# Layer statistics taken behind the additions that finish x, in a block of twelve sublayers

## The chip, the cores and the metric

The kernel runs on one core of one Trainium2 chip. The metric is the device time in microseconds (us). The core has five engines that work side by side, each through its own queue of instructions in order: PE (matrix products and transposes), DVE (vector operations), ACT (activation functions, each from a table that has to be loaded), POOL (general vector work) and SP (which here only issues transfers). They wait for one another through semaphores. On-chip data lie in SBUF, and what PE writes lies in PSUM. An array holds 128 rows (partitions); a tile is 128 tokens.

## What is computed

A perceiver-like stack of four levels, each with a cross attention to a context of 1601 tokens, an attention among the 64 tokens of a sequence, and a feed-forward layer. The twelve sublayers differ (slot attention with a GRU cell, random-feature attention, mixtures of experts, a quantised product at the end), but all are joined in one way:

```python
def _layernorm(x, axis=-1, eps=1e-05):
    m = jnp.mean(x, axis=axis, keepdims=True)
    v = jnp.var(x, axis=axis, keepdims=True)
    return (x - m) / jnp.sqrt(v + eps)

    # x: (16, 64, 256) float32
    x = x + _L1_xattn_ref(_layernorm(x, axis=-1), ctx_1024, ...)
    x = x + _L1_attn_ref(_layernorm(x, axis=-1), ...)
    x = x + _L1_ffn_ref(_layernorm(x, axis=-1), ...)
    ...
```

So every sublayer needs mean and variance of each of 1024 rows of 256 numbers, and these are known only when the sublayer before has added its result to x.

## The kernel before

x stays in SBUF through all layers, as `self.x` of shape 128 x 8 x 256: eight tiles of 128 tokens. The layers are methods that run one after the other: `l0_xattn`, `l0_attn`, `l0_ffn`, `l1_xattn` and so on to `l3_attn`, which carries the last feed-forward layer in its loop. Each layer adds its result to x tile by tile. In l1_attn, l2_xattn, l2_attn and l3_xattn this is `add_to_x` (line 358, DVE, out of PSUM). In l1_xattn it is an addition on POOL in `end` (line 1320). In l1_ffn it is a DVE addition in `refine` (line 1690), and in l2_ffn a multiply-and-add per expert in `weighted_experts` (line 879), of which the last expert's finishes x.

At its head a layer normalises x, per tile: `bn_stats` and `bn_aggr` on DVE give mean and variance; `rstd` makes the factor out of the variance with a tensor_scalar on DVE (line 133, variance plus eps), Sqrt on ACT (line 134) and a reciprocal on DVE (line 135), for two or four tiles at a time; another tensor_scalar writes the norm, (x - mean) * factor, to `xln` (in l1_ffn to `xi`). PE then transposes the norm, DVE and ACT in turn copy the transposes from PSUM to `xT` (lines 124 and 126; cT in l1_ffn), and the layer's first product (`lin_t`, `lin` or `gelu_t`) reads that.

The heads that matter here: `linear` in `token_attention` (line 2488 on), which serves l1_attn and l3_attn and takes the tiles in two halves of four; `start` in l1_ffn (line 1552), also by halves; `layernorm` (line 138), called by l2_xattn and l2_ffn for all eight tiles; `linear` in l2_attn (line 1829); `prepare` in l3_xattn (line 2048).

Some other instructions stand in the neighbourhood. `token_attention` clears its array `vm` with a POOL memset (line 2491), fills the small array `ones` (lines 2494 and 2496), and POOL later adds the norm and a bias row to x (lines 2524 and 2525). In l3_attn the product `pb` (line 2202) and 32 small additions `bias` (line 2212) make the position bias. In l2_xattn's streamed loop DVE masks the scores (line 1779), ACT squares them (lines 1781 and 1782) and POOL adds up some of the exponent's results, `tot` (line 2385). In l2_attn's loop over tiles, DVE makes `kp` (line 1910), `rec` (lines 1941 and 1942) and `kv` (lines 1925 and 1926), and POOL scales `qp` once (line 1896).

What sets the order: in the layers here, PE's instructions and some others that are marked with `pin` keep the order of the program. All others, the statistics, factors and norms among them, are placed by a planner, which goes by costs of its own and by when operands are due; so the order on DVE, ACT and POOL can differ from that of the code. The compiled order is what the prediction goes by.

Of the kernel before, what the change touches and what calls it, by code (L numbers as in the profile page):

```python
# [64 lines left out]
class Sections:  # L65
# [21 lines left out]

    def c(self, name):
        lo, n = CONSTS_AT[name]
        return self.cst[:, lo : lo + n]  # L90
# [37 lines left out]
    def rstd(self, pool, var, eps, tag, scale=1.0):  # L128
# [7 lines left out]
        return r  # L136

# [732 lines left out]
    def weighted_experts(self, ps, sb2, xT, comb, n, hidden, down):  # L870

        nc = self.nc
        for e in range(n):
# [4 lines left out]
            def evac(t, pm):  # L878
                nc.vector.scalar_tensor_tensor(
                    self.x[:, t, :], pm, comb[:, t, e : e + 1], self.x[:, t, :], ALU.mult, ALU.add  # L880
                )

# [128 lines left out]
    def l1_xattn(self):  # L1011
# [3 lines left out]
        with ExitStack() as ctx:  # L1015
# [301 lines left out]
            def end(step, after):  # L1317
                s, i = step
                if i == 2:
                    pin(nc.gpsimd.tensor_tensor(self.x[:, s.t, :], self.x[:, s.t, :], s.s, ALU.add))  # L1320
                if after and after[1] == 0:
# [29 lines left out]
            for n in range(len(a)):  # L1351
# [12 lines left out]
                else:  # L1364
                    for x in sb_.p:
                        x.exp()
                        x.weigh()
                update(sb_, an and an[0])
# [91 lines left out]
    def l1_ffn(self):  # L1460
# [3 lines left out]
        with ExitStack() as ctx:  # L1464
# [214 lines left out]
            def refine(s):  # L1679
                fT = sb.tile([P, 4, N], F32, tag=f"eT{s.i}", name="fT")  # L1680
                for c in range(4):
                    gelu_t(fT[:, c, :], fw1, s.cT, self.v(k + "refine_b1")[:, c : c + 1], KC, c * P)
                for t in range(TT):
# [6 lines left out]
                    nc.vector.tensor_tensor(s.x[:, t, :], s.x[:, t, :], y, ALU.add)  # L1690

# [36 lines left out]
    def l2_xattn(self):  # L1728
        nc, tc, d = self.nc, self.tc, self.d
        with ExitStack() as ctx:  # L1730
# [10 lines left out]
            self.layernorm(sb, self.x, xln)  # L1741
# [46 lines left out]
            def out(t):  # L1788
# [3 lines left out]
                self.add_to_x(t, pm)  # L1792

            self.stream(ps, sb2, load, wkv[:, :, :D], wkv[:, :, D:], copy, weights, finish, out)

    def l2_attn(self):
        nc, tc, d = self.nc, self.tc, self.d
        F, HT = 64, NT // 2
        with ExitStack() as ctx:
# [27 lines left out]
            def linear(i):  # L1827
# [993 lines left out]
```

## Time and profile before

| | |
|---|---|
| median of 3 runs | 3760.18 us (3752.28 to 3766.32) |
| profiled execution | 3753.96 us |
| its span | 3752.2 us |
| PE busy | 3440.3 us, 92% |
| DVE busy | 1974.1 us, 53% |
| ACT busy | 1451.3 us, 39% |
| POOL busy | 1291.0 us, 34% |
| granted TensorE clock, mean | 0.959 |

Times in the profile are microseconds from the start of the span. A line of the timeline has the start, the busy time, the engine, the line of the code, the operation, the arrays (out<-in) with their shapes, the number of instructions put together in the line (x), and in brackets the idle time before it and what ended it. Operations of l1_xattn run up to 1917 us, l1_attn to 2005, l1_ffn to 2333, l2_xattn to 2996, l2_attn to 3103, l2_ffn to 3467, l3_xattn to 3621, and l3_attn from there.

### The profile page before, as it was taken

Reading aid. Unit: us, or ns where it says so; the run is one execution under the profiler, and the core shown is the slowest. Engines: PE = TensorE matmul, PEld = TensorE weight load, DVE = VectorE, ACT = ScalarE, POOL = GpSimd, SP = SyncE. Lnnn points to the kernel's source line nnn. Section 1 sums busy time; section 2 is a strip of 40 time slices with the busy share of each in tenths; the row PEclk is TensorE's granted clock in tenths of the full one; section 3 lists DMA queues with packets and bytes.
Section 4 is the critical chain, followed back from the end, with each engine's and each line's share of the span. In section 5 each row is a group of like instructions: output and inputs, shape, how many; then the busy total and the mean of one; then the engine's idle time right before and its main releaser. Section 6 shows DMA issues by size and latency. Waiting matters only on the chain.

```text
span 3752.2 us, 70803 instructions
## 1 busy us (share of the span) xinstructions
PE 3440.3 (92%) x30966; PEld 2187.8 (58%) x30966; DVE 1974.1 (53%) x3676; ACT 1451.3 (39%) x2076; POOL 1291.0 (34%) x787
## 2 busy tenths in 40 slices
PE   8999999996999969999977988999999789999986
PEld 4555555563665645555545666667767555555554
DVE  5344333436555546656657554577767665333346
ACT  2333333333444414444423443466666612111213
POOL 1555555562011123333321001577777630000012
PEclk9999999998999979999989999999999989999997
DMA  4111001101332344343101001111111004111640
GB/s 145 38 38 38 31 27 38 38 10 35 105 96 87 111 158 163 127 146 110 37 26 40 1 6 44 68 56 38 56 38 38 11 2 174 43 36 30 278 180 13
DMA packets 106123, 258.66 MB, mean 69 GB/s; under 512 B 9203, under 2 KB 74483, under 8 KB 103510
## 3 DMA queue, kind: packets, MB, share of 16 engines
q1 hardware_dynamic: 97366, 222.68, 16.6%
q10 hardware_dynamic: 6912, 27.27, 2.3%
q8 instruction: 243, 3.98, 0.4%
q0 software_dynamic: 1536, 4.20, 0.4%
q14 instruction: 66, 0.54, 0.0%
HBM read 248.34 MB, written 5.77 MB: 68 GB/s over the span
## 4 chain that ended last, share of the span: by engine, by line
PE 77%; DVE 12%; ACT 7%; issue 2%; DMA 1%; POOL 1%; SPq 0%; ACTq 0%; DVEq 0%; POOLq 0%
PE sc L2452 15%; PE pk L2452 15%; PE lin L2452 7%; PE acc L2452 6%; PE lin_t L2452 5%; ACT e L327 5%; PE pu L2452 4%; PE lin L194 3%; PE gate L2017 3%; PE up L2017 3%; PE pc L1639 3%; PE prz L2452 2%; PE gelu_t L1549 2%; PE turn L2457 2%; PE pa L2452 1%
## 5 line engine op out<-in xcount | busy, mean ns | idle before, releaser
L2385 POOL TENSOR_TENSOR tot<-tot,e 128x1024 f32<-128x1024 f32 (+1 forms) x340 | 802.9, 2361 | 374.5 <-ACT e L327 251.2
L270 DVE TENSOR_REDUCE m<-sc 128x4 f32<-128x2048 f32 x96 | 220.1, 2293 | 271.3 <-PE sc L2452 270.2
L1779 DVE SCALAR_TENSOR_TENSOR e<-sc,row_L_xattn_nbias,free 128x2048 f32<-128x2048 f32 x104 | 244.3, 2349 | 121.8 <-PE sc L2452 116.3
L1781 ACT ACTIVATE e<-e 128x2048 f32<-128x2048 f32 x104 | 198.7, 1910 | 243.2 <-DVE e L1779 243.2
L327 ACT ACTIVATE e<-sc 128x2048 f32<-128x2048 f32 x104 | 195.2, 1877 | 241.2 <-PE sc L2452 239.6
L2452 PE MATMUL sc<-qb,kT 32*128 32x128 f32 x6656 | 244.8, 283 | 36.6 <-DVE m L284 12.3
L2452 PEld LDWEIGHTS sc<-qb,kT 32*128 32x128 f32 x6656 | 205.9, 187 | 80.6 <-issue 24.5
L2452 PE MATMUL acc<-e,v 128*32 128x128 f32 x6656 | 226.6, 276 | 6.4 <-ACT e L1782 6.4
L2452 PEld LDWEIGHTS acc<-e,v 128*32 128x32 f32 x6656 | 170.3, 110 | 105.7 <-issue 95.1
L2452 PE MATMUL pk<-cT,wk 128*128 128x512 f32 (+1 forms) x512 | 207.0, 534 | 3.6 <-DVE rows L300 3.6
L2452 PE MATMUL pk<-wv,cT 128*128 128x256 f32 x832 | 209.8, 394 | 0.0
L1782 ACT ACTIVATE e<-e 128x2048 f32<-128x2048 f32 x104 | 198.7, 1911 | 3.3
L2452 PE MATMUL pk<-cT,wkv 128*128 128x512 f32 (+1 forms) x512 | 197.2, 526 | 0.0
L2452 PE MATMUL pk<-wkv,cT 128*128 128x256 f32 x832 | 196.3, 386 | 0.0
L2452 PEld LDWEIGHTS pk<-wv,cT 128*128 128x128 f32 x832 | 149.7, 190 | 75.5 <-issue 58.2
L2452 PEld LDWEIGHTS pk<-wkv,cT 128*128 128x128 f32 x832 | 153.3, 190 | 28.3 <-issue 4.3
L1639 PE MATMUL pc<-ew,eh 128*128 128x256 f32 x640 | 158.8, 391 | 0.0
L2452 PE MATMUL pu<-cn,e 128*64 128x257 f32 (+1 forms) x1248 | 146.5, 391 | 12.9 <-POOL e L1186 12.9
L2452 PE MATMUL sc<-kT,qb 32*128 32x512 f32 (+2 forms) x1536 | 140.8, 465 | 14.9 <-DVE m L270 2.3
L2021 ACT ACTIVATE g<-gate 128x512 f32<-128x512 f32 x68 | 40.6, 597 | 292.2 <-PE gate L2017 292.2
L1176 POOL TENSOR_TENSOR e<-e,mx 128x512 f32<-128x512 f32 x96 | 81.8, 883 | 194.7 <-DVE mx L1175 194.7
L2022 DVE TENSOR_TENSOR hT<-up,g 128x512 f32<-128x512 f32 x68 | 47.0, 692 | 178.8 <-PE up L2017 174.6
(519 smaller groups left out, 6339.5 us busy)
## 6 DMA issues: line engine op xcount, KB each, us to landing
cT<-in_ctx_t SPq DMA_DIRECT2D x128, 832.0 KB, 6.1
cn<-in_ctx_n SPq DMA_DIRECT2D x32, 1664.0 KB, 12.6
piece<-in_ctx_n ACTq DMA_DIRECT2D x32, 640.0 KB, 3.9
w<-in_L_attn_W SPq DMA_DIRECT2D x8, 1024.0 KB, 7.2
piece<-in_ctx_n ACTq DMA_DIRECT2D x16, 384.0 KB, 3.5
w<-in_L_ffn_W SPq DMA_DIRECT2D x16, 256.0 KB, 4.8
down<-in_L_ffn_w_down SPq DMA_DIRECT2D x16, 256.0 KB, 2.7
gate<-in_L_ffn_w_gate SPq DMA_DIRECT2D x16, 256.0 KB, 2.7
```

Of the source, the lines that this page charges most:

```text
L194: nc.tensor.matmul(pm, xT[:, k, t * P : (t + 1) * P], w[:, k, :], start=(k == 0), stop=(k == kc - 1))
L270: nc.vector.tensor_reduce(x.m4[:, g, :, i], pm, AX.X, ALU.max)
L327: nc.scalar.activation(e, pm, AF.Exp, scale=0.25)
L1176: pin(nc.gpsimd.tensor_tensor(p.e, p.e, p.mx.unsqueeze(2).to_broadcast(p.shape), ALU.subtract))
L1549: nc.tensor.matmul(pm, w[:, c, lo : lo + m], cT[:, c, :], start=(c == 0), stop=(c == nk - 1))
L1639: nc.tensor.matmul(pc[:, n, j, :], s.eh[i][:, c, tok], ew2[:, c, cols], start=False, stop=(c == 3))
L1779: nc.vector.scalar_tensor_tensor(e16, pm16, nb, free[:, at : at + P].unsqueeze(1).to_broadcast([P, 16, P]), ALU.add, ALU.mult)
L1781: nc.scalar.activation(e, e, AF.Relu)
L1782: nc.scalar.activation(e, e, AF.Square)
L2017: nc.tensor.matmul(pm[-1], w[:, k, n * P : (n + 1) * P], xT[:, k, tok], start=(k == 0), stop=(k == KC - 1))
L2385: nc.gpsimd.tensor_tensor(tot[:w], x.first if c == 1 else tot[:w], e[:w], ALU.add)
L2452: ins = self.nc.tensor.matmul(*args, **kw)
```

## The change

Two arrays are kept for the whole run: `xm` (mean and variance of each tile) and `xr` (the factors). `measured(t)` takes the statistics of tile t of x and is called directly behind the addition that finishes this tile, in seven layers. `factors(lo, hi)` makes the factors of some tiles. Unless told otherwise, measured calls it for two tiles whenever the second of a pair is done; in l1_xattn, l1_attn and l3_xattn tiles 0 to 5 are done at once behind tile 5, and in l1_ffn tiles 0 to 3 in the second half's refine. `normed(t, to)` writes the norm. The seven layers behind lose their statistics and call normed only. In token_attention the memset of vm is moved, in the code, behind the first half's transposes.

```diff
+        self.xm = self.const.tile([P, NT, 2], F32, tag="xm", name="xm")
+        self.xr = self.const.tile([P, NT], F32, tag="xr", name="xr")
...
+    def measured(self, t, root=True):
+
+        nc = self.nc
+        st = self.const.tile([P, 6], F32, tag="x_st", name="x_st", bufs=2)
+        nc.vector.bn_stats(st, self.x[:, t, :])
+        nc.vector.bn_aggr(self.xm[:, t], st)
+        if root and t % 2:
+            self.factors(t - 1, t + 1)
+
+    def factors(self, lo, hi):
+        nc = self.nc
+        r = self.xr[:, lo:hi]
+        nc.vector.tensor_scalar(r, self.xm[:, lo:hi, 1], 1.0, 1e-5, ALU.mult, ALU.add)
+        nc.scalar.activation(r, r, AF.Sqrt)
+        nc.vector.reciprocal(r, r)
+
+    def normed(self, t, to):
+        self.nc.vector.tensor_scalar(to, self.x[:, t, :], self.xm[:, t, 0:1], self.xr[:, t : t + 1], ALU.subtract, ALU.mult)
... weighted_experts (l2_ffn)
+                if e == n - 1:
+                    self.measured(t)
... l1_xattn
                     pin(nc.gpsimd.tensor_tensor(self.x[:, s.t, :], self.x[:, s.t, :], s.s, ALU.add))
+                    self.measured(s.t, s.t == NT - 1)
...
+                    self.factors(0, NT - 2)
... l1_ffn, start and refine
-                mv = sb2.tile([P, TT, 2], F32, tag="ln_mv", name="ln_mv")
                 for t in range(TT):
-                    st = sb2.tile([P, 6], F32, tag="ln_st", name="ln_st", bufs=3)
-                    nc.vector.bn_stats(st, s.x[:, t, :])
-                    nc.vector.bn_aggr(mv[:, t, :], st)
-                r = self.rstd(sb2, mv[:, :, 1], 1e-5, "ln_r")
-                for t in range(TT):
-                    nc.vector.tensor_scalar(
-                        s.xi[:, t, :], s.x[:, t, :], mv[:, t, 0:1], r[:, t : t + 1], ALU.subtract, ALU.mult)
+                    self.normed(s.i * TT + t, s.xi[:, t, :])
...
+                if s.i:
+                    self.factors(0, TT)
...
                     nc.vector.tensor_tensor(s.x[:, t, :], s.x[:, t, :], y, ALU.add)
+                    self.measured(s.i * TT + t, s.i == 1)
... l2_xattn and l2_ffn, head
-            self.layernorm(sb, self.x, xln)
+            for t in range(NT):
+                self.normed(t, xln[:, t, :])
... l2_xattn and l2_attn, output
                 self.add_to_x(t, pm)
+                self.measured(t)
... l3_xattn, output
                 self.add_to_x(s.t, pm)
+                self.measured(s.t, s.t > 5)
+                if s.t == 5:
+                    self.factors(0, 6)
... token_attention (l1_attn, l3_attn); the heads of l2_attn and l3_xattn change in the same way, but have no memset
-        nc.gpsimd.memset(vm, 0.0)
...
-            mv = sb2.tile([P, HT, 2], F32, tag="ln_mv", name="ln_mv")
-            for t in range(HT):
-                st = sb2.tile([P, 6], F32, tag="ln_st", name="ln_st", bufs=3)
-                nc.vector.bn_stats(st, x[:, t, :])
-                nc.vector.bn_aggr(mv[:, t, :], st)
-            r = self.rstd(sb2, mv[:, :, 1], 1e-5, "ln_r")
...
-                    nc.vector.tensor_scalar(
-                        xln[:, t + j, :], x[:, t + j, :], mv[:, t + j, 0:1], r[:, t + j : t + j + 1],
-                        ALU.subtract, ALU.mult)
+                    self.normed(i * HT + t + j, xln[:, t + j, :])
...
+            if i == 0:
+                nc.gpsimd.memset(vm, 0.0)
...
             self.add_to_x(t, pm)
+            if then is None:
+                self.measured(t, t > 5)
+                if t == 5:
+                    self.factors(0, 6)
```

More of the change, by code (lines that the diff above doesn't have):

```diff
@@ L1950, in project @@
                 self.add_to_x(t, pm)
+                self.measured(t)
             self.pinned = True
@@ L1986, in l2_ffn @@
             xT = sb.tile([P, KC, T], F32, tag="xT", name="xT")
-            self.layernorm(sb, self.x, xln)
+            for t in range(NT):
+                self.normed(t, xln[:, t, :])
             self.transpose(ps, xln, xT)
@@ L2049, in prepare @@
                 xln = sb.tile([P, HT, D], F32, tag="xln", name="xln")
-                mv = sb2.tile([P, HT, 2], F32, tag="ln_mv", name="ln_mv")
-                for t in range(HT):
-                    st = sb2.tile([P, 6], F32, tag="ln_st", name="ln_st", bufs=3)
-                    nc.vector.bn_stats(st, x[:, t, :])
-                    nc.vector.bn_aggr(mv[:, t, :], st)
-                r = self.rstd(sb2, mv[:, :, 1], 1e-5, "ln_r")
                 xT = sb.tile([P, KC, 512], F32, tag="xT", name="xT")
@@ L2059, in prepare @@
                     for j in range(2):
-                        nc.vector.tensor_scalar(
-                            xln[:, t + j, :], x[:, t + j, :], mv[:, t + j, 0:1], r[:, t + j : t + j + 1],
-                            ALU.subtract, ALU.mult)
+                        self.normed(i * HT + t + j, xln[:, t + j, :])
                         for c in range(KC):
@@ L2504, in linear @@
             xln = sb.tile([P, HT, D], F32, tag=f"xln{i}", name="xln")
-            mv = sb2.tile([P, HT, 2], F32, tag="ln_mv", name="ln_mv")
-            for t in range(HT):
-                st = sb2.tile([P, 6], F32, tag="ln_st", name="ln_st", bufs=3)
-                nc.vector.bn_stats(st, x[:, t, :])
-                nc.vector.bn_aggr(mv[:, t, :], st)
-            r = self.rstd(sb2, mv[:, :, 1], 1e-5, "ln_r")
             xT = sb.tile([P, KC, 512], F32, tag=f"xT{i}", name="xT")
@@ L2514, in linear @@
                 for j in range(2):
-                    nc.vector.tensor_scalar(
-                        xln[:, t + j, :], x[:, t + j, :], mv[:, t + j, 0:1], r[:, t + j : t + j + 1],
-                        ALU.subtract, ALU.mult)
+                    self.normed(i * HT + t + j, xln[:, t + j, :])
                     for c in range(KC):
```

## The prediction

> **What bounds the kernel now.** I read the head of the page first, for the size of things, then the shares of the chain of waits, then the timeline around each of the seven places where one layer ends and the next normalises x.
>
> ```profile
> span 3752.2 us, 70803 instructions
> PE 3440.3 (92%) x30966; PEld 2187.8 (58%) x30966; DVE 1974.1 (53%) x3676; ACT 1451.3 (39%) x2076; POOL 1291.0 (34%) x787
> ...
> PE 77%; DVE 12%; ACT 7%; issue 2%; DMA 1%; POOL 1%; SPq 0%; ACTq 0%; DVEq 0%; POOLq 0%
> ```
>
> PE is the bound; only some 300 us of the span are PE idle. The change takes nothing from PE, so it can win only in the short stretches where PE stands still at a layer's head. At the seven heads, from the last addition to the first product that needs the transposed norm, they are 5 to 14 us long and partly filled. Half a percent, about what a measurement of this kernel can tell from no change, is 18.8 us.
>
> Timeline, head of l1_attn. POOL's memset of vm runs 3.51 us, and a DVE instruction on 4 numbers per partition takes 2.15 us beside it; the same one takes 0.15 us alone (at 3468.85, for instance). The transposes wait for the norm, lin_t for the copy behind it.
>
> ```profile
> 1917.50 3.51 POOL L2491 MEMSET vm<- 128x4096 f32 x1
> 1918.98 2.15 DVE L133 TENSOR_SCALAR ln_r<-ln_mv 128x4 f32<-128x4 f32 x1
> 1922.47 4.03 DVE L2515 TENSOR_SCALAR xln<-x,ln_mv,ln_r 128x256 f32<-128x256 f32 x6
> 1922.91 1.97 PE L2457 MATMUL tr<-cst,xln 128*128 128x128 f32 x8 [8.79 <-DVE xln L2515]
> 1927.25 2.05 PE L2452 MATMUL lin_t<-xT,wqkv 128*128 128x512 f32 x2 [2.37 <-DVE xT L124]
> ```
>
> Timeline, end of l2_xattn and the token loop of l2_attn. POOL adds exponentials 2.43 us each without a pause; the copy L2311 takes 1.60 us beside them and 0.29 without. In l2_attn POOL has two instructions of 5.4 us back to back (the boundary is at 3073.1), and the addition to tile 1 falls into the second; kp behind it releases PE's pk.
>
> ```profile
> 2963.43 12.14 POOL L2385 TENSOR_TENSOR tot<-tot,e 128x1024 f32<-128x1024 f32 x5
> 2969.25 1.60 DVE L2311 TENSOR_TENSOR xT<-half 128x128 f32<-128x128 f32 x1
> 2993.49 0.29 DVE L2311 TENSOR_TENSOR xT<-half 128x128 f32<-128x128 f32 x1
> 3067.70 10.81 POOL L1896 TENSOR_SCALAR qp<-qp 128x2048 f32<-128x2048 f32 x2 [11.53 <-ACT qp L1895]
> 3074.13 0.42 DVE L358 TENSOR_TENSOR x<-lin,x 128x256 f32<-128x256 f32 x1 [0.58 <-PE lin L2452]
> 3075.33 1.23 DVE L1910 TENSOR_SCALAR kp<-pkp 128x1024 f32<-128x1024 f32 x1 [0.77 <-PE pkp L2452]
> 3076.61 1.98 PE L2452 MATMUL pk<-va,kp 64*128 64x33 f32 x32
> ```
>
> Timeline, end of l3_xattn. The memset runs ten microseconds before the last addition, hurting nobody. pb starts when that addition is done; 32 small DVE additions follow pb, then the copy, then lin_t.
>
> ```profile
> 3607.17 3.51 POOL L2491 MEMSET vm<- 128x4096 f32 x1 [6.76 <-DMA hot<-in_buckets]
> 3617.54 0.15 POOL L2494 MEMSET ones<- 128x64 f32 x1 [6.86 <-PE pa L2452]
> 3620.18 0.42 DVE L358 TENSOR_TENSOR x<-lin,x 128x256 f32<-128x256 f32 x1 [1.97 <-PE lin L2452]
> 3620.66 6.41 PE L2202 MATMUL pb<-emb,hot 32*128 32x16 f32 x128 [0.52 <-DVE x L358]
> 3629.41 4.53 DVE L2212 TENSOR_TENSOR bias<-pb,cst 64x64 f32<-64x64 f32 x32
> 3634.80 2.90 PE L2452 MATMUL lin_t<-xT,wqkv 128*128 128x512 f32 x3 [5.83 <-DVE xT L124]
> ```
>
> **The rule that speaks against the change.** The row says 0.15 us for a factor instruction. The Trainium skill ("SBUF — State Buffer", section "Who interferes with whom") says that a DVE tensor_scalar between SBUF tiles in a two-port mode, or a DVE operation with two SBUF inputs, shares one pair of ports with GpSimd: whoever starts first keeps it for the whole instruction and the other stands still. The rows above agree (2.15 against 0.15, 1.60 against 0.29), and a reciprocal (L2303, 1.75 us with or without POOL) or an operation out of PSUM is spared. The old code did such work in heads where POOL is mostly idle; the new code puts factors() and normed() where POOL is busy. By the row alone the sum below would be 18.6 us of gain; by the rule it is 3. I take the rule, place by place.
>
> **Part by part.** No instruction is new in kind: 56 bn_stats (0.31 to 0.39 us), 56 bn_aggr (0.08 behind another) and the norms (0.33 to 0.36) are only moved; the factors become pairs or (0,6)+(6,8), some dozen more small DVE and ACT operations. PE's instructions are the same, but for local order in l1_ffn, l2_xattn and l2_ffn. No DMA is added; SP swaps five weight and context loads in l2_ffn, far ahead of their use.
>
> l1_xattn to l1_attn: in the loop bn_stats waits for POOL's addition (0.72 us) with den or sr behind it on DVE; 3.2 us of DVE idle lie there (waiting for pu), so I charge 0.3. In the head, the memset was moved down in the code, but in the compiled order POOL still runs it right behind the addition, before the first norm. So the norms, ready at 1918.0, start at 1921.2; five of them (1.8), the copy (0.7), and lin_t comes at 1924.05 instead of 1927.25, because the copy now stands ahead of the norm that POOL's x+=xln (2.44) blocks. +3.2 - 0.3 = +2.9.
>
> l1_attn to l1_ffn: bn_stats and bn_aggr, 0.4 a tile, in a loop where DVE idles 0.26 to 2.8 a tile: 0.4 in all; the reciprocal of (0,6) waits for ACT's Sqrt table (load 1.28, from 1999.70) with rec of tile 7 behind it: 0.5. In the head xi starts at 2006.1 instead of 2009.51; the fifth stands behind POOL's addition to 2010.2, and gelu_t starts at 2011.3 instead of 2014.62: 3.3. The planner also reorders the control part of l1_ffn (bias preparation later, routing earlier), which I count as 0, bounds -2 and +2. Sum +2.4.
>
> l1_ffn to l2_xattn: two more table loads (2.56) inside refine hide behind PE's gelu products; DVE needs 1.95 a tile against PE's 1.73, so the last addition is 0.45 late. All eight norms follow at once: lin_t at 2338.8 instead of 2344.5, of which 3.4 were PE work (pk) that now comes behind it: +2.3.
>
> l2_xattn to l2_attn: the factor of (0,1) falls into a POOL addition (to 2959.85) with the reciprocal and the exponent's input L1779 behind it, for which ACT and then PE wait: -2.0. That of (2,3), between the two half operations, waits about 1; the copy L2311 then meets the next POOL addition: about -2 more. In the head the four norms follow L2311 directly, without 3.4 us of statistics, 2.3 us of lock at 3000.24 and a second Sqrt: +4.2. Sum 0 (bounds -4 and +4).
>
> l2_attn to l2_ffn: DVE is the bound of this loop (busy without a gap 3079 to 3091, 5.3 us a tile), so what is added counts in full: tiles 0 and 1 0.4 each ahead of kp; tiles 2 to 5 0.4 each, less 0.5 of slack, plus 0.3 for each of two pairs of factors: 1.7. The factor of (0,1), ready at 3075.0, waits for POOL's qp to 3078.5: 3.5, with kp, and so PE's pk, behind it. Sum -6.0. The head begins 2.4 earlier, but all eight norms now stand before the first copy, and ACT drops one Sqrt load: +1.6. Sum -4.4 (bounds -7 and 0).
>
> l2_ffn to l3_xattn: additions come every 0.865, taking 0.48; 0.4 of statistics and at times 0.3 of factors fit, POOL is idle. First norm 3467.4; the copy of two tiles to 3469.6, the fourth norm, ACT's copy, lin_t at 3471.25 instead of 3474.06: +2.8.
>
> l3_xattn to l3_attn: the loop has idle DVE (0). But the memset is now behind ones on POOL, which waits for the last pa: it runs 3617.7 to 3621.2, just when six norms stand in DVE's queue ahead of the last addition. Five end at 3623.0, the sixth waits for POOL's x+=row (2.45) to 3625.4, the addition ends at 3625.8 instead of 3620.6, and pb, bias (needs all of pb) and lin_t follow: pb to 3632.3, bias to 3636.8, copy 0.7, lin_t 3637.7: -3.0 (without the lock +2.1).
>
> Sum: 2.9+2.4+2.3+0-4.4+2.8-3.0 = +3.0 us. From the profiled execution's 3754.0 (span 3752.2 and 1.8 around it) that is 3751.0; it lies 6.2 below the median of the runs, 3760.2, inside their 3752.3 to 3766.3. The forecast for the median is 3757.
>
> **Rivals.** *Faster:* the locks fall elsewhere (POOL a few us earlier or later, in l2_attn above all) and the cheap rows hold: l1_attn 5.9, l1_ffn 2.4, l2_xattn 2.3, l2_attn 4.2, l2_ffn -1.1, l3_xattn 2.8, l3_attn 2.1, together 18.6: 3741.6, and PE staying clocked up over the shorter gaps (its products run at half pace for some 4 us at 1927 and 3474) could add 1 or 2 a head: 3735. Against it: the blocked rows above. *Slower:* bn_stats behind POOL's addition in l1_xattn. If that addition has the multiplications of the other half (three of 1.04 and one of 0.40) ahead of it, DVE stands 3.5 us in each of 8 tiles with den and sr behind it: 28 us, 3785. It decides from 2.7 us a tile on. For it: POOL is pinned and busy there; against it: in the last tile they end at 1902.6, and the addition comes at 1916.84. *The change doesn't do what it says:* that is so for the memset, and is in the sum; would it run behind the transposes after all, the last head gains 5 and the first 2.5: 3750.
>
> **How the numbers follow.** Little change, 0.76; the locks missing, or clock gained, so that over 0.5% is won, 0.16; the l1_xattn stall or more blocked places, over 0.5% lost, 0.08. The bounds of the places (5 of them by 2 to 4 us) combine to about 8, the scatter of the runs is 7: near 3757 that is 3744 to 3770; to leave out no more than 2 in 10 I reach towards both rivals: 3739 to 3775.
>
> **What would show it.** In the changed kernel's timeline: a factor instruction of 3 us or more near 3075, one of 1 to 2 us near 2958; the memset between ones and the first norm at both heads; the last addition of l3_xattn some 5 us after its product; lin_t of l3_xattn 4.5 us after the last addition. The prediction is wrong if the factor instructions are all near 0.15 us (faster), or bn_stats in l1_xattn has idle over 2 us before it that POOL ends (slower).

## The result, and the profile after

The changed kernel takes 3751.9 us (median of 16 runs, 3748.7 to 3758.3) beside 3758.6 us of the kernel before (16 runs, 3752.0 to 3766.4). The ratio is 0.9981, with a 95% interval of 0.9972 to 0.9989: a gain of 0.1 to 0.3%, under the half per cent that I had set as the bound of "no change". The forecast was 3757 and "little change"; the forecast gain was 3.0 us, and 6.7 came.

The page of the changed kernel shows the bound where it was: PE is busy for 92% of the span, as before, and DVE has 10 us more, among them the instructions that stand still beside POOL (called locked in what follows).

```profile
span 3753.9 us, 70772 instructions
PE 3443.9 (92%) x30951; PEld 2189.3 (58%) x30966; DVE 1983.8 (53%) x3682; ACT 1452.0 (39%) x2079; POOL 1292.3 (34%) x787
...
PE 76%; DVE 13%; ACT 7%; issue 3%; POOL 1%; DMA 0%; another core or an unknown queue 0%; SPq 0%; ACTq 0%; DVEq 0%; POOLq 0%
```

This profiled execution is not shorter than the one before (span 3753.9 against 3752.2). It was 3.2 us late when it came to the first head, before any head had changed. The shift arises near 1411, where l1_xattn begins, and is 3.46 or 3.47 us at the additions of that layer's first seven tiles and 3.18 at the last. It is not the change: from the layer's first `qT` to its first addition to x the old kernel took 115.9 us in one profile and 119.1 in another, the changed one 119.6 here. So what follows compares stretches, not spans.

Timeline of the changed kernel, head of l1_attn (start, busy time, engine, line, operation, arrays). POOL starts the memset of vm 0.41 us ahead of the first norm, and the norm, which takes 0.38 without it, stands 3.34. lin_t comes 7.28 us after the last `s` of l1_xattn is written; before it was 10.49.

```profile
1920.77 3.51 POOL L2527 MEMSET vm<- 128x4096 f32 x1
1921.18 3.34 DVE L158 TENSOR_SCALAR xln<-x,xm,xr 128x256 f32<-128x256 f32 x1
1924.53 0.38 DVE L158 TENSOR_SCALAR xln<-x,xm,xr 128x256 f32<-128x256 f32 x1
...
1927.22 1.22 PE L2465 MATMUL lin_t<-xT,wqkv 128*128 128x512 f32 x1 [0.68 <-ACT xT L129]
```

Timeline, end of l2_xattn. One factor instruction stands 1.91 us beside POOL's additions, a second one 0.72, and the copy behind it meets the next addition and stands 2.26 us (0.29 alone). The exponent's input, L1802, waits behind it, then ACT 4.60, then PE 4.32. In the profile before, where this copy stood 1.60, PE waited 2.41 at the same place (last line).

```profile
2953.95 1.91 DVE L153 TENSOR_SCALAR xr<-xm 128x2 f32<-128x2 f32 x1
2967.00 0.72 DVE L153 TENSOR_SCALAR xr<-xm 128x2 f32<-128x2 f32 x1
2968.01 2.26 DVE L2324 TENSOR_TENSOR xT<-half 128x128 f32<-128x128 f32 x1
2970.19 2.34 DVE L1802 SCALAR_TENSOR_TENSOR e<-sc,row_L_xattn_nbias,free 128x2048 f32<-128x2048 f32 x1
2972.56 1.91 ACT L1804 ACTIVATE e<-e 128x2048 f32<-128x2048 f32 x1 [4.60 <-DVE e L1802]
2972.58 2.09 PE L2465 MATMUL sc<-qb,kT 32*128 32x128 f32 x32 [4.32 <-DVE e L1802]
```

```profile
2973.17 1.84 PE L2452 MATMUL sc<-qb,kT 32*128 32x128 f32 x32 [2.41 <-DVE e L1779]
```

Timeline, tile 1 of l2_attn. The factor instruction starts inside POOL's second qp and ends with it, at 3078.4; kp ends with it, and PE's pk waits 2.03 us for kp.

```profile
3067.58 10.81 POOL L1912 TENSOR_SCALAR qp<-qp 128x2048 f32<-128x2048 f32 x2 [15.85 <-ACT qp L1911]
3074.30 0.42 DVE L380 TENSOR_TENSOR x<-lin,x 128x256 f32<-128x256 f32 x1 [0.58 <-PE lin L2465]
3075.44 2.97 DVE L153 TENSOR_SCALAR xr<-xm 128x2 f32<-128x2 f32 x1
3076.59 1.82 DVE L1926 TENSOR_SCALAR kp<-pkp 128x1024 f32<-128x1024 f32 x1
3078.49 3.40 PE L2465 MATMUL pk<-va,kp 64*128 64x33 f32 x32 [2.03 <-DVE kp L1926]
```

Timeline, end of l3_xattn. The memset stands behind `ones`; a cast, a small addition and six norms are held beside it and beside POOL's row addition, and the last addition to x starts 5.99 us after its product does (1.17 us before the change). pb, bias and lin_t follow.

```profile
3614.77 3.51 POOL L2527 MEMSET vm<- 128x4096 f32 x1
3614.97 3.39 DVE L2239 CAST identb<-cst 128x128 bf16<-128x128 f32 x1
3615.18 6.96 DVE L158 TENSOR_SCALAR xln<-x,xm,xr 128x256 f32<-128x256 f32 x6
3616.06 1.13 PE L2465 MATMUL lin<-wv,hT 128*128 128x256 f32 x4 [0.52 <-ACT hT L2159]
3622.05 0.41 DVE L380 TENSOR_TENSOR x<-lin,x 128x256 f32<-128x256 f32 x1
3622.52 7.33 PE L2215 MATMUL pb<-emb,hot 32*128 32x16 f32 x128 [5.33 <-DVE x L380]
3635.30 2.04 PE L2465 MATMUL lin_t<-xT,wqkv 128*128 128x512 f32 x2 [3.56 <-DVE xT L127]
```

The stretches from the first head to the end in one table (us; read off the timelines, from start to start where nothing else is said; plus is a gain). "Before" and "after" are the profiled executions of the two kernels. The prediction's terms stand in the same order. The marks are instructions by the name of the array that they write: an exponent input is the mask operation on DVE that writes `e` (L1802; there are seven in the tail), the last `rec` is L2315, and the second `z` is the second addition to `z` in l2_attn (L1880).

| stretch | before | after | gain | predicted |
|---|---|---|---|---|
| l1_attn head: last s written to lin_t | 10.49 | 7.28 | +3.2 | +3.2 |
| l1_attn loop: lin_t to last addition | 77.34 | 78.14 | -0.8 | -0.9 |
| l1_ffn head: last addition to gelu_t | 10.03 | 5.56 | +4.5 | +3.3 |
| l1_ffn loop: gelu_t to last addition | 317.69 | 319.22 | -1.5 | -0.45 |
| l2_xattn head: last addition to lin_t | 12.20 | 7.65 | +4.6 | with the next row +2.75 |
| l2_xattn loop: lin_t to the seventh last exponent input | 605.26 | 607.94 | -2.7 | |
| l2_xattn tail: from there to the last rec | 40.83 | 44.29 | -3.5 | -4 |
| l2_attn head: rec to the second z | 16.68 | 12.34 | +4.3 | +4.2 |
| l2_attn, second z to addition of tile 1 | 66.85 | 71.94 | -5.1 | -0.8 |
| l2_attn, additions of tile 1 to 7 | 28.14 | 33.11 | -5.0 | -5.2 |
| l2_ffn head: last addition to router product | 5.53 | 3.96 | +1.6 | +1.6 |
| l2_ffn loop: router product to last addition | 358.43 | 357.60 | +0.8 | 0 |
| l3_xattn head: last addition to lin_t | 7.83 | 4.41 | +3.4 | +2.8 |
| l3_xattn loop: lin_t to last transposes | 144.00 | 141.73 | +2.3 | 0 |
| l3_attn head: last transposes of l3_xattn to lin_t | 16.74 | 20.19 | -3.5 | -3.0 |
| l3_attn, lin_t to the end | 117.35 | 118.60 | -1.3 | none |

The heads repeat within 0.4 us in the other profiles of these two kernels, which come below; the loops do not, and the last row lies between 113 and 119 in fourteen profiles, in no order by kernel.

The one large row that I had not seen coming is the stretch in l2_attn ahead of tile 1's addition. Only the statistics of tile 0 are new in it, yet it took 5.1 us longer, all of it in PE's own busy time: 56.9 against 51.6 us for the same products. The experiments begin with the rows that were foreseen and then turn to that one. Single edits here move the whole by a few microseconds, and the intervals of all variants of the changed kernel but one overlap that of the change as made (0.9972 to 0.9989). What they show, they show in the stretches.

### The profile page after: what moved, and what is told of

It is laid out like the page before. It is cut to its first block, busy times and chain, and to the rows that moved or that the text cites. A ratio compares the mean times of both kernels' runs of the same rounds, so it can differ in the third digit from the quotient of the medians.

```text
span 3753.9 us, 70772 instructions
## 1 busy us (share of the span) xinstructions
PE 3443.9 (92%) x30951; PEld 2189.3 (58%) x30966; DVE 1983.8 (53%) x3682; ACT 1452.0 (39%) x2079; POOL 1292.3 (34%) x787
## 4 chain that ended last, share of the span: by engine, by line
PE 76%; DVE 13%; ACT 7%; issue 3%; POOL 1%; DMA 0%; another core or an unknown queue 0%; SPq 0%; ACTq 0%; DVEq 0%; POOLq 0%
PE sc L2465 15%; PE pk L2465 15%; PE lin L2465 7%; PE acc L2465 6%; PE lin_t L2465 5%; ACT e L349 4%; PE pu L2465 4%; PE gate L2035 3%; PE up L2035 3%; PE lin L216 3%; PE pc L1658 3%; PE prz L2465 2%; PE turn L2470 2%; PE gelu_t L1575 2%; PE pa L2465 1%
## 5 line engine op out<-in xcount | busy, mean ns | idle before, releaser
L1802 DVE SCALAR_TENSOR_TENSOR e<-sc,row_L_xattn_nbias,free 128x2048 f32<-128x2048 f32 x104 | 244.3, 2349 | 115.6 <-PE sc L2465 114.0
L2465 PE MATMUL sc<-cT,qT 128*64 128x512 f32 (+1 forms) x768 | 141.9, 522 | 3.6 <-ACT scs L1180 3.1
```

Source lines behind the costliest of these rows:

```text
L1802: nc.vector.scalar_tensor_tensor(e16, pm16, nb, free[:, at : at + P].unsqueeze(1).to_broadcast([P, 16, P]), ALU.add, ALU.mult)
L2465: ins = self.nc.tensor.matmul(*args, **kw)
```

## Experiments

The theory is that what the change wins at the heads it gives back where its small instructions meet POOL (factors in l2_xattn and l2_attn, norms beside the memset). The rivals are that the statistics in the loops cost what is missing, whatever POOL does, and, for l2_attn, that the new order makes PE slow.

### The factors made late

```diff
 l2_xattn and l2_attn, output
-                self.measured(t)
+                self.measured(t, t > 5)
+                if t == 5:
+                    self.factors(0, 6)
```

> The changed kernel, with the factors of l2_xattn and l2_attn made for tiles 0 to 5 at once behind tile 5, when POOL is idle, instead of pair by pair. Theory (the shared port lock on the factor instruction): in l2_xattn, from the mask operation that starts at 2945.73 in the changed kernel to the last rec the time goes from 44.3 us back to about 41 (it was 40.8 before the change); in l2_attn, from the addition to tile 1 to that of tile 7, from 33.1 to about 29.6 (28.1 before); together -6.7 us, about 3745. Rival (the statistics load DVE, the lock is incidental): both stay within 1 us of the changed kernel, no change in the total.

Measured: 3745.25 us, ratio 0.9973 (0.9964 to 0.9983). l2_xattn's tail is 40.53 us, as expected. From the timeline of this kernel:

```profile
2960.60 1.41 DVE L2328 TENSOR_TENSOR xT<-half 128x128 f32<-128x128 f32 x1
2969.51 0.17 DVE L153 TENSOR_SCALAR xr<-xm 128x6 f32<-128x6 f32 x1
```

The factor takes 0.17 us, and the copy stands 1.41, much as it did before the change (1.60). The statistics are still in the loop. The length of the whole tail alone would not settle it, since two later profiles of the old kernel have 42.67 and 43.25 us there (the second with added products far ahead). But their excess lies behind the fifth of the seven exponent inputs, where PE runs at half clock for 13 and 12 us instead of 7. From the first to the fifth, which waits behind the copy, all eight profiles without pairs of factors take 20.9 to 21.0 us, the four of the old order among them, and the four that have the pairs and the held copy 24.4 or 24.5. So the 3.5 us were the factors' lock and its sequel, and the rival is out for this place. The sequel is the larger part, and it depends on where POOL stands: in two later kernels that keep the pairs (memset put back, refine undone) the same factors stand 1.9 and 0.5 us, but the copy behind them only 0.29, and the fifth exponent input comes after 22.5 us. That is 1.5 us for the lock and 2.0 for the sequel. In l2_attn the expectation failed: additions of tile 1 to 7 took 31.93 us, not 29.6, although no factor stood. The table on the clock, further down, tells why a single profile of that stretch can't be read by itself.

### Eps moved into the square root

```diff
 factors
-        nc.vector.tensor_scalar(r, self.xm[:, lo:hi, 1], 1.0, 1e-5, ALU.mult, ALU.add)
-        nc.scalar.activation(r, r, AF.Sqrt)
+        nc.scalar.activation(r, self.xm[:, lo:hi, 1], AF.Sqrt, bias=self.eps)
```

> The changed kernel with eps added by ACT, as the bias of Sqrt, so that the factor's tensor_scalar on DVE is gone everywhere and only Sqrt and the reciprocal are left, pair by pair as in the changed kernel. Theory (the lock): the same two intervals as with late factors shrink, 44.3 to about 42 and 33.1 to about 29.9; all other heads within 0.4 us of the changed kernel; total about -6, 3746. Rival (ACT's wait in the midst of the stream, or the reciprocal that waits for it, is what costs): the intervals stay above 43.5 and 32.

Measured: 3746.36 us, ratio 0.9977 (0.9968 to 0.9986); tail of l2_xattn 40.87. The pairs stay where they are in the code, only the DVE instruction that can be locked is gone. The fifth exponent input comes 21.0 us behind the first, as without pairs. That is a second, independent way to the same 3.5 us: it was this instruction, not the number or the place of the pairs. In l2_attn's head this kernel took 15.16 us instead of 12.34; the cause was not followed up.

### The memset put back, and the memset alone

The first is the changed kernel with the memset at its old place; the second is the kernel before with only the memset moved.

```diff
 token_attention, ahead of the loops / behind the transposes of a half
+        nc.gpsimd.memset(vm, 0.0)
...
-            if i == 0:
-                nc.gpsimd.memset(vm, 0.0)
```

> The changed kernel with the memset of vm back at its old place in the code. Theory (the memset holds the ports while six norms stand ahead of the last addition): in l3_xattn's end the memset runs some ten microseconds earlier, the last addition starts near 2 us after its product instead of 4.9, and from the last pa product to lin_t it takes about 23 us instead of 26.6 (23.2 before the change); l1_attn's head stays at 7.3 us from the last GRU operation to lin_t. Total -3.7 us, about 3748. Rival (the order of the norms ahead of the addition is what costs, memset or not): it stays above 25.5 us.

> The kernel before with only the memset of vm moved behind the first half's transposes in the code. Theory (the moved memset costs only because norms now stand ahead of the last addition): in l3_xattn's end only the cast of identb is held, the last addition is about 1 us late and lin_t about 1 us late (24.2 us from the last pa product instead of 23.2); l1_attn's head within 0.3 us; total +1, 3760. Rival (the memset there costs by itself): lin_t is 3 us late or more, 3762 and above.

Measured: put back, 3746.64 us, ratio 0.9976 (0.9966 to 0.9986), and l3's last transposes to lin_t 17.38 instead of 20.19. In its timeline the memset runs at 3599.78, ten microseconds ahead of the six norms, and these end in 4.13 us instead of 6.96. Alone, 3756.68 us, ratio 1.0003 (0.9994 to 1.0013), and the same stretch 17.00 against 16.74 before. So moving the memset costs 2.8 us with the norms waiting there and 0.3 without, and the norms alone cost 0.6 (17.38 against 16.74): neither part is dear alone, the pair is. (The 0.6 is a balance that was not taken apart: with the memset put back the last addition still comes 2.0 us later than before, and pb takes 7.36 us instead of 6.41, but bias starts as soon as pb ends, where it came 2.3 us behind it.) In the head of l1_attn putting it back changes nothing (7.18 against 7.28), because POOL runs it right behind the last addition in either order, as the prediction had read from the compiled order.

### The memset really moved out of the way

```diff
 l3_xattn, output
-                self.measured(s.t, s.t > 5)
-                if s.t == 5:
-                    self.factors(0, 6)
+                self.measured(s.t, False)
+                if s.t == NT - 1:
+                    self.factors(0, NT)
 token_attention
+        if not own_input:           # l3_attn
+            nc.gpsimd.memset(vm, 0.0)
...
+            if i == 0 and own_input:    # l1_attn, behind POOL's two additions
+                keep(last)
+                keep(nc.gpsimd.memset(vm, 0.0))
```

`keep` holds an instruction to the order of the program, and `last` is POOL's addition of the bias row. The kernel also has the late factors of the first experiment.

> The changed kernel with e1's late factors in l2_xattn and l2_attn, and two more edits: the memset of vm runs before the last tile in l3_xattn and behind the first half's additions of the last tile in l1_xattn, and l3_xattn makes its factors once behind the last tile. Theory of the shared path (the memset held the factor and the first norms, 3.3 to 3.5 us in each head): l1_attn head, last u behind s to lin_t, falls from 7.3 to about 4; l3 from the last transposition to lin_t falls from 20.2 to about 14.4; l2_xattn's tail stays at 40.5; the time is about 3745.2 - 3.2 - 5.8 = 3736. Rival (the memset in its later place blocks the norms behind it or the v writes all the same): the heads gain less than 1 us each and the time stays at 3743 to 3746.

Measured: 3743.24 us, ratio 0.9955 (0.9940 to 0.9970). It is faster than the kernel before, and its interval lies just below that of the change as made (0.9972 to 0.9989). But 3736 was expected, and the time is the rival's. The timeline of this kernel at the head of l1_attn:

```profile
1920.55 0.41 DVE L158 TENSOR_SCALAR xln<-x,xm,xr 128x256 f32<-128x256 f32 x1
1923.66 5.76 PE L2469 MATMUL lin_t<-xT,wqkv 128*128 128x512 f32 x8 [0.68 <-ACT xT L129]
1924.85 5.75 DVE L158 TENSOR_SCALAR xln<-x,xm,xr 128x256 f32<-128x256 f32 x1
1926.95 3.51 POOL L2539 MEMSET vm<- 128x4096 f32 x1
1932.51 3.70 PE L2469 MATMUL lin_t<-xT,wqkv 128*128 128x512 f32 x8 [3.10 <-ACT qb L2548]
```

The first norm takes 0.41, and lin_t comes 4.36 us after s, as expected (7.28). But the memset now stands behind POOL's additions, and the second half's norm at 1924.85 is held by an addition and then by the memset, to 1930.6. qb stands behind it on DVE, and PE waits 3.10 us for qb. The loop takes 80.61 instead of 78.14 us, and of 2.9 us gained 2.5 are gone. In l3 the stretch from the last transposes to lin_t fell from 20.19 to 15.38; of the microsecond missing to 14.4, 0.9 is PE's, which ran pb in 7.33 us instead of 6.41. So theory and rival were each right at one of the two places: in l3 the path is free, in l1_attn the block has moved to the norms behind the memset.

### The refine's statistics undone

```diff
 l1_ffn, refine; l2_xattn, head
-                if s.i:
-                    self.factors(0, TT)
...
-                    self.measured(s.i * TT + t, s.i == 1)
...
-            for t in range(NT):
-                self.normed(t, xln[:, t, :])
+            self.layernorm(sb, self.x, xln)
```

> The changed kernel with the statistics of l1_ffn's refine and of l2_xattn's norm as before the change (behind the layer, in layernorm). If the statistics between the product and POOL's multiplication cost 1.5 us of the loop: l1_ffn from gelu_t to the last addition 317.7 instead of 319.2 us. The head of l2_xattn goes back from 7.65 to about 12 us, and lin_t to the seventh last exponent input from 607.9 to 605.3; the sum is 4.55 - 1.5 - 2.7 = 0.4 us slower at most: 3752. If the reordered control part is what costs, the loop stays at 319.2.

Measured: 3748.48 us, ratio 0.9976 (0.9967 to 0.9985). The loop takes 317.43 us again, so the reordered control part costs nothing in it and the statistics cost the 1.5 to 1.8. The timeline of the changed kernel shows how (two lines of the kernel before stand below it):

```profile
2323.45 0.43 DVE L1711 TENSOR_TENSOR x<-x,y 128x256 f32<-128x256 f32 x1 [0.81 <-POOL y L1710]
2323.91 0.43 DVE L145 BATCH_NORM_STATS2 x_st<-x 128x6 f32<-128x256 f32 x1
2324.37 0.18 DVE L146 BATCH_NORM_AGGREGATE xm<-x_st 128x2 f32<-128x6 f32 x1
2324.47 0.39 DVE L1709 TENSOR_TENSOR y<-po,row_L_ffn_router_b 128x256 f32<-128x256 f32 x1
2325.01 0.64 POOL L1710 TENSOR_TENSOR y<-y,row_L_ffn_router_b 128x256 f32<-128x256 f32 x1 [1.59 <-DVE y L1709]
2325.68 0.42 DVE L1711 TENSOR_TENSOR x<-x,y 128x256 f32<-128x256 f32 x1 [0.82 <-POOL y L1710]
```

```profile
2327.12 0.43 DVE L1690 TENSOR_TENSOR x<-x,y 128x256 f32<-128x256 f32 x1 [0.82 <-POOL y L1689]
2328.85 0.42 DVE L1690 TENSOR_TENSOR x<-x,y 128x256 f32<-128x256 f32 x1 [0.82 <-POOL y L1689]
```

A tile goes from DVE (y) to POOL and back to DVE (x), with the next y behind x on DVE. The statistics stand between x and the next y, and DVE stands idle 0.82 us for POOL all the same: a tile takes 2.23 us where it took 1.73. From the first to the last of the four additions it is 6.7 or 6.8 us in all eight profiles with these statistics and 5.2 in all six without. The head is 11.06 us against 7.65, and the l2_xattn loop 604.49 against 607.94, each some 0.8 us less than expected. From gelu_t to the seventh last exponent input that is 933.0 us undone, 934.8 as changed and 935.1 before: this part of the change was worth 0.3 us, where I had summed +2.3. The other profiles lie at 935.1 to 935.7 (changed, without added products) and at 934.9 and 935.2 (old), so 0.3 is not told from nothing. That the undone kernel is some 2 us faster there than the old one, with the old statistics in both, is not explained; the head of l2_xattn (11.06 against 12.20) and its loop (604.49 against 605.26) have most of it.

The last kernel puts the same edit on top of the late memset and late factors.

> The kernel with the late memset and the late factors (3743.2) and, besides, the refine's statistics back behind the layer. If the parts add up, the stretch from gelu_t of l1_ffn to the seventh last exponent input of l2_xattn is 1.8 us shorter, as it was alone (933.0 against 934.8), and all else is the same: 3741.4, ratio about 0.995. If that stretch was only a matter of the clock's phase: 3743 or more.

Measured: 3743.78 us, ratio 0.9966 (0.9955 to 0.9977). The stretch is 933.0 us against 935.1 of the kernel without the edit, as expected, but the time as a whole did not fall: 3743.2 and 3743.8, with overlapping intervals. That is the time of the other expectation (3743 or more). Two microseconds in one place are at the limit of what these runs can tell, and the claim that the edit helps the whole is not shown.

### The slow stretch in l2_attn

Is it the new order, or something that comes and goes? First both kernels again as they are.

> The changed kernel as it is, another execution, to see whether the stretch of l2_attn from the second z to the last addition of tile 1 is the same from one execution to the next. If the slower TensorE there is bound to the changed order: 72 us again, and clock 0.76 to 0.77. If it is the phase at which the clock gate's window falls: anything from 67 to 72.

> The kernel before as it is, another execution. Bound to the order: 66.8 us for the same stretch, clock 0.83, as in its two other profiles of the same code there. Phase: anything from 67 to 72.

Measured: the changed kernel 3751.78 us (ratio 0.9987, 0.9970 to 1.0004) and 71.97 us for the stretch; the kernel before 3760.99 us (ratio to itself 0.9999, 0.9988 to 1.0011), and in this execution 71.98 us, with nothing changed. Busy time by window of the old kernel, first the profiled execution shown so far, then this one; the second window of each begins some 37 us behind the second z and goes to the addition of tile 1 (columns: window, its length, busy time of PE, weight loads, DVE, ACT and POOL, granted clock, share of the DMA engines, GB/s):

```profile
3007.00:3044.00 37.00, 26.65 (x202) 15.57 (x201) 15.89 (x26) 8.81 (x11) 14.60 (x4) 0.77 0.01 2
3044.00:3074.00 30.00, 24.95 (x316) 17.61 (x316) 19.30 (x35) 7.47 (x8) 10.10 (x4) 0.92 0.01 1
```

```profile
3014.00:3051.00 37.00, 26.63 (x201) 15.38 (x200) 15.84 (x26) 8.76 (x11) 14.61 (x4) 0.77 0.01 2
3051.00:3086.00 35.00, 30.26 (x320) 21.66 (x320) 19.56 (x35) 7.53 (x8) 10.71 (x4) 0.77 0.00 1
```

The same products take 30.3 us of PE instead of 25.0, at a granted clock of 0.77 instead of 0.92. PE's rows there, first of the execution shown so far and then of this one, show where it begins: up to the eight transposes all is the same, gaps too; then 32 pk take 3.63 us, where 28 of them took 1.75.

```profile
3056.78 0.66 PE L2457 MATMUL tr<-cst,z 128*128 128x128 f32 x4 [0.81 <-DVE qn L124]
3058.20 1.35 PE L2457 MATMUL tr<-cst,z 128*128 128x128 f32 x8 [0.77 <-ACT nT L126]
3059.49 1.75 PE L2452 MATMUL pk<-va,kp 64*128 64x33 f32 x28
```

```profile
3063.84 0.66 PE L2457 MATMUL tr<-cst,z 128*128 128x128 f32 x4 [0.81 <-DVE qn L124]
3065.26 1.65 PE L2457 MATMUL tr<-cst,z 128*128 128x128 f32 x8 [0.77 <-ACT nT L126]
3066.84 3.63 PE L2452 MATMUL pk<-va,kp 64*128 64x33 f32 x32
```

Cut into slices of 3.4 us, the granted clock of every profile is 1.00 or 0.50 but for slices in which it changes, so it steps between full and half on a grid of about this width. Three slices of the first profile of the old kernel, from 6.8 us behind the second z on (the clock is the third number from the end):

```profile
3014.08:3017.48 3.40, 0.98 (x8) 0.74 (x8) 2.67 (x5) 1.54 (x3) 0.00 (x0) 1.00 0.00 0
3017.48:3020.88 3.40, 1.17 (x6) 1.17 (x7) 0.12 (x2) 0.00 (x0) 1.93 (x1) 0.56 0.00 0
3020.88:3024.28 3.40, 2.82 (x12) 0.91 (x10) 0.67 (x1) 1.10 (x2) 0.00 (x0) 0.50 0.00 0
```

That fits a rule of the Trainium skill ("TensorE: Matmul & The Clock Gate", section "The HAM clock gate"), by which the activity window is 3.4 us and free-running. Where this grid lies against the program is called the phase in what follows. By the theory of the phase, the same gaps can or can't cost a step, by where the grid falls. To move the program against the grid, products were added far ahead, at the start of l2_xattn:

```diff
 lin_t, called by l2_xattn with more=2 or 3
+                if n == 0 and h == 0:
+                    for _ in range(more):
+                        nc.tensor.matmul(pm, w[:, 0, :P], xT[:, 0, :512], start=True, stop=True)
```

> The changed kernel with two extra products of 128x512 ahead of the first lin_t of l2_xattn, written over by it (they leave nothing behind): everything after is about 0.9 us later, and nothing else differs. Phase theory: TensorE's clock steps on a grid of about 3.4 us that doesn't follow the program, so the first step down behind the second z of l2_attn comes 0.9 us earlier, at about 10.7 instead of 11.56 us behind it; there the kernel before had 66.85 us from the second z to the addition of tile 1, so about 67 us instead of 72 and the time some 4 us less in spite of the added work. Theory that the changed order slows TensorE: 72 us as before, time 0.9 us more.

> The same with three extra products, about 1.3 us. Phase theory: first step down at about 10.25 us behind the second z, between the kernel before (10.6, 66.85 us) and the changed kernel with the memset put back (9.8, 71 us): either 67 or 71 us. Order theory: 72 us.

> The kernel before with three extra products in the same place, about 1.3 us. Phase theory: the step down moves from 10.6 to 9.3 (or one grid step later, 12.7) us behind the second z, away from the one place where 66.85 us was seen: about 71 to 72 us without any of the change, and the time 5 us up or more. Order theory: 66.85 us, time up by 1.3 us.

Measured: 3749.3 us (ratio 0.9984), 3753.2 (0.9995) and 3763.6 (1.0021, 1.0013 to 1.0029). All three missed in detail, because the phase can't be set in that way: it differs between two executions of one kernel too (10.6 and 11.2 us for the old one in the table). But each profile shows its own phase, and this table over all fourteen is the yield. The second column is the time from the second z to the first step down of the clock, worked out from the clock of 3.4 us slices (a slice of 0.56 is at full clock for 12% of it: 3.12 x 3.4 = 10.6).

| kernel | first step down, us | second z to addition of tile 1 | additions 1 to 7 |
|---|---|---|---|
| changed, refine undone | 9.7 | 70.89 | 30.02 |
| changed, memset back | 9.8 | 70.96 | 30.02 |
| before, memset alone | 10.5 | 66.85 | 28.10 |
| before | 10.6 | 66.85 | 28.14 |
| changed, late memset, refine undone | 10.9 | 71.93 | 29.55 |
| before, again | 11.2 | 71.98 | 31.40 |
| changed, 3 products | 11.2 | 71.94 | 33.89 |
| changed | 11.6 | 71.94 | 33.11 |
| changed, again | 11.6 | 71.97 | 33.12 |
| changed, eps on ACT | 11.8 | 72.64 | 32.38 |
| changed, late memset | 11.9 | 72.54 | 31.91 |
| changed, late factors | 12.0 | 72.59 | 31.93 |
| changed, 2 products | 12.2 | 70.33 | 29.88 |
| before, 3 products | 12.4 | 70.47 | 27.73 |

The time of the stretch (third column) goes with the phase and not with the kernel. Where old and new order meet at one phase they agree: 71.98 and 71.94 at 11.2, 70.47 and 70.33 at 12.4 and 12.2. Only a narrow part, near 10.5, gives 66.85 (9.8 and 10.9 on either side give 71.0 and 71.9), and the profile before had fallen into it. The order theory is out: the old order has 70 to 72 us in two of four profiles.

The last column, read at equal phase, gives what the change costs there: 33.89 against 31.40, 29.88 against 27.73, so 2.2 to 2.5 us. How much of that is the lock shows in the start of PE's pk behind the addition to tile 1. At 11.2 it comes 2.93 us behind it in the old kernel and 4.00 in the changed one with three products:

```profile
3086.01 0.42 DVE L358 TENSOR_TENSOR x<-lin,x 128x256 f32<-128x256 f32 x1 [0.57 <-PE lin L2452]
3088.94 3.63 PE L2452 MATMUL pk<-va,kp 64*128 64x33 f32 x32
```

```profile
3079.17 0.42 DVE L383 TENSOR_TENSOR x<-lin,x 128x256 f32<-128x256 f32 x1 [0.58 <-PE lin L2468]
3080.31 2.78 DVE L153 TENSOR_SCALAR xr<-xm 128x2 f32<-128x2 f32 x1
3083.17 3.63 PE L2468 MATMUL pk<-va,kp 64*128 64x33 f32 x32 [1.00 <-DVE kp L1929]
```

In the other pair it is 2.93 and 3.63. So the lock made pk 1.1 and 0.7 us late, although the factor stood 2.78 and 2.42; in the old kernel PE was still busy with acc when kp was ready. The statistics of the later tiles are left with 1.4 us in both pairs. The kernels without the lock and with the statistics (late factors, eps on ACT) also have 2.93.

Two things stay open. None of the ten profiles of the new order met the narrow good part, and two of the four of the old one did (one of them with the memset moved); whether the change has made this rarer, or it was chance, is not settled. And the old kernel with three products lost 6.8 us in the median of 17 runs, where the products are worth 1.3: that would fit a phase that most of its executions share, which was not seen run by run.

## Why the prediction was right, and where not

"Little change", put at 0.76, was right, and so was the mechanism; 3757 was forecast and 3751.9 measured. Six heads gain 21.6 us, and the head of l3_attn and the loops, with their locks and statistics, take most of it back. With the l2_attn loop taken at equal phase (-2.3) and the stretch ahead of it at nothing, the rows for which the prediction has a term other than 0 sum to 3.2 - 0.8 + 4.5 - 1.5 + 4.6 - 2.7 - 3.5 + 4.3 - 2.3 + 1.6 + 3.4 - 3.5 = +7.3 us, and the medians differ by 6.7. That they lie so near each other is in part luck: the other three rows would add 1.8, and they vary with the clock. The nearness of the time is luck in part too. Two terms were wrong by -2.0 and +3.7 us and partly cancel, and of the 5.1 us between forecast and result 1.5 come from the base, a median of three runs (3760.2) where sixteen gave 3758.6.

*The rule of the shared ports, taken place by place.* Right. All that I had named is in the trace: the memset between ones and the first norm at both heads, a factor of 2.97 us near 3075, one of 1.91 near 2954, the last addition of l3_xattn some 5 us late, lin_t of l3_xattn 4.4 us after the last addition. The row alone (0.15 us) would have given 18.6 us of gain. Two kernels in which the factor no longer meets POOL have l2_xattn's tail back at 40.5 and 40.9. How much a lock costs is another matter: it hung on what its sequel met. The prediction states the rule too widely in one respect: by the Trainium skill ("SBUF — State Buffer", section "Who interferes with whom"), a DVE instruction with two SBUF inputs contends only with a GpSimd instruction that reads SBUF. The memset reads nothing, and `bq`, a DVE operation of that kind, took 0.14 us beside it at 1921.12. Nothing in the sum hangs on this.

*l1_xattn's loop, and the slower rival.* It costs nothing: the shift against the profile before is 3.46 or 3.47 us at seven of its tiles and 3.18 at the last. The rival's 3.5 us a tile did not come.

*The faster rival's clock.* It had PE stay clocked up over a shorter gap at 1927 and 3474. At 1927 it did not; at 3474 it did here: the first eight lin_t of l3_xattn take 3.70 us instead of 5.97, which is the 2.3 us of that loop's row. Five of the ten profiles of the new order have this (141.7 us for the loop), the other five 143.4 to 144.2, and the four of the old order 143.8 to 146.1.

*l1_attn, l2_attn's head, l2_ffn's head.* Within 0.2 us each.

*l1_ffn's head.* +4.5 instead of +3.3. The fifth norm did stand behind POOL's addition, as said, but the first copy ran ahead of it and only one was left behind it. The head of l3_xattn, too, gained more than forecast, 3.4 instead of 2.8.

*l1_ffn to l2_xattn, +2.3.* This step failed in size: +0.3, not told from nothing. "DVE needs 1.95 a tile against PE's 1.73, so the last addition is 0.45 late" counted DVE's busy time. What sets the pace there is a round trip, DVE to POOL and back, with 0.82 us of waiting for POOL that the statistics don't fill: 2.23 us a tile, and 1.5 late.

*l2_attn's loop, -6.0.* This step failed in size too: -2.2 to -2.5 at equal phase. "DVE is the bound of this loop, so what is added counts in full" charged 0.8 for tiles 0 and 1, where the runs show nothing, 1.7 for the tiles behind, where they show 1.4, and 3.5 for the lock. The instruction did stand 2.97 us, but PE, busy with acc in the meantime, had pk only 1.1 or 0.7 us later than without it. The statement took one stretch of dense DVE work, 3079 to 3091, for the whole loop.

*The memset in l3, -3.0.* Measured -3.5, and 2.8 of it by undoing it.

*"If the memset ran behind the transposes after all, the last head gains 5 and the first 2.5."* The kernel that does so gained 4.8 and 2.9 there, and lost 2.5 of the latter again in l1_attn's loop, since the second half's norms stand behind it.

*The base of the sum.* Summing against the profiled execution was sound only for places that don't depend on the clock's phase. From the last s to l3_attn's v product, two profiles of the old kernel take 1727.4 and 1737.7 us, a difference of 10.3 in one and the same program, and the changed kernel 1724.2 and 1724.3, but 1737.2 with the three added products, which are worth 1.3.

## What to carry to other kernels

Work taken out of the critical head and put into a loop is free only if it does not meet an engine beside which its own engine stands still, as DVE did here beside POOL: look up, for each moved instruction, what POOL does at the very time when it will be issued, who stands behind it in its queue, and whether the engine that waits at the end would have been busy anyway. In a loop that goes back and forth between two engines, the round trip counts, and an engine with idle time in it may still have no room. And a difference of a few microseconds between two profiles is read at equal phase of the clock, or from medians; one profile of each kernel would here have shown the change as a loss.

## What was not expected of the hardware

TensorE's clock steps between full and half on a grid of about 3.4 us that is tied neither to the program nor, from one execution to the next, to its start. In l2_attn, where three gaps of 0.8 to 1.0 us follow one another in 5 us, the stretch took 66.9 us at one phase and 70.3 to 72.6 at the others for the same products. A memset on POOL, which reads nothing, holds a norm or a cast on DVE for its whole remaining length (3.34 us and 3.39 us beside 3.51), but not bn_stats, which took its 0.43 us at 1920.78 beside it, nor bq, a product of two small arrays in SBUF (0.14 us at 1921.12).
